# The convolution layer's load of t's rows, issued by SyncE instead of ScalarE

## The chip, the cores and the metric

The kernel runs on one core of a Trainium2 chip. A core has five engines that run side by side: TensorE (PE, with its weight loads PEld), VectorE (DVE), ScalarE (ACT), GpSimd (POOL) and SyncE (SP), which here only issues DMAs. Each engine works through its own queue of instructions in order and waits on semaphores for the others. SyncE, ScalarE and GpSimd can issue DMAs; a DMA that waits for something keeps all that stands behind it in that engine's queue waiting too. The metric is the device time of one execution in microseconds, the median of several runs.

## The reference

A feature map x of 1 x 256 x 256 x 128 float32 runs through four residual layers, each applied to a group-normalised input: triangle attention, two triangle multiplications, and a convolution layer. The change lies in the last, whose reference is

```python
def c1(t):   # a 1 x 9 convolution along a row, 128 channels to 1
    return lax.conv_general_dilated(t, w1, (1, 1), 'SAME', dimension_numbers=DN) + b1
def c2(t):   # a 128 x 128 product per pixel
    return jnp.einsum('bhwc,cd->bhwd', t, w2c) + b2
t = relu(c1(x))
y = jnp.concatenate([x[:, :1], x[:, 1:] + t[:, :-1]], axis=1)
u = relu(c1(y))
z_main = u + jnp.roll(y, 1, axis=1)
z = jnp.concatenate([z_main[:, :H - 2], u[:, H - 1:H] + y[:, H - 2:H - 1], y[:, H - 1:H]], axis=1)
v = relu(c2(z))
p = jnp.concatenate([z[:, :, :1], z[:, :, 1:] + v[:, :, :-1]], axis=2)
r = relu(c2(p))
q_main = r + jnp.roll(p, 1, axis=2)
```

The images t and u have one channel: each value is added to all 128 channels of a pixel. The output is x + q.

## The kernel before, in words

The first three layers end at about 2925 us; what follows is the convolution layer. It works on 32 groups of 8 image rows, channels on the partitions (1 MB a group). `for s in range(NR + 2)` at L1695 holds the order of all instructions, written out by hand; nothing is reordered by a planner.

Per group s, the main work is: `load9` (L1462) brings x into one of nine buffers; ScalarE writes x, scaled and moved by a row, into PSUM (`start_z`, L1580, tile `p_zp`, for group s + 1) and a copy of x into `p_q` (L1704); VectorE adds the one-channel part to make `p_z` (`finish_z`, L1595); TensorE multiplies by w2c twice (`p_half` and `q_half`, both L1601), VectorE takes the products (L1609, L1623), GpSimd adds the row-shifted p (`residual`, L1615 to L1617); `emit` transposes the group two steps back on TensorE (L1638, tile `p_pt`), ScalarE copies it out of PSUM (L1639, `p_o`) and SyncE stores it (L1640).

The one-channel images t and e (e is what u and t together add to a group's rows) are made in 16 blocks of 16 rows, one block per two groups, some groups ahead of their use. `taps` (L1468 on TensorE, `p_st` on ScalarE at L1472) makes the nine products of the 1 x 9 convolution, and SyncE writes them to DRAM with four DMAs (`sD`, L1477). `load_block` (L1487, two DMAs on SyncE) reads them back shifted so that adding nine numbers gives c1(x). A block b then passes these steps over two groups:

- even group: `sum_taps` on VectorE (L1509, L1510), `relu_t` on ScalarE (L1515), `shift_t` on GpSimd (L1519, L1522), and `keep_t` (L1527), a DMA from GpSimd's queue that writes t's rows to DRAM (`tD`).
- odd group: `load_t` (L1531), which reads t's rows back, one row up, into `p_t2`; `image_u` on VectorE (L1536), `relu_u` on ScalarE (L1540), `image_e` on GpSimd (L1545, which needs `p_t2`), and `keep_e` (L1551), a DMA from GpSimd's queue that writes e's rows to DRAM (`eD`).
- next even group: `load_e` (L1564), two DMAs from ScalarE's queue that read e's rows as single-partition rows; GpSimd broadcasts them to all partitions (`spread_e`, L1572) for `finish_z`.

So `load_t` must wait until the DMA of `keep_t` has landed, and `load_e` until that of `keep_e` has. In the profile the DMA issues of these queues show as SPq, ACTq and POOL. The PSUM tiles `p_zp`, `p_pp` (of `taps`) and `p_pt` share two buffers in turn, so the second `p_pt` of a group waits for `p_st` to free the buffer of `p_pp`.

The first three blocks are made ahead of or inside groups 0 and 1 with their DMAs on SyncE (`begin_image`, `end_image`); the loop's own loads of t are in the thirteen odd groups 3 to 27. `taps` runs in the loop's groups 2 to 25 and the x loads end with group 23's.

In an odd group before the change the queues hold, in this order:

- SyncE: x load of group s + 8, four `sD` writes, two `p_S` loads, output store.
- ScalarE: `p_pb` column, `p_zp`, `p_q`, **load_t**, `p_st`, two `p_o` copies, `relu_u`, a last column of `p_q`.
- GpSimd: `residual`, `spread_e`, `image_e`, the write of e.

Of the kernel before, what the change touches and what calls it, by code (L numbers as in the profile page):

```python
# [32 lines left out]
def kernel(ctx: ExitStack, tc: tile.TileContext, a: dict, out: bass.AP):  # L33
    nc = tc.nc
# [33 lines left out]
    tD = dram.tile([1, (N + 2) * NP], F32, name="tD")  # L68
# [1032 lines left out]
    with tc.tile_pool(name="x5", bufs=7) as x5_pool, tc.tile_pool(name="p5", bufs=2) as sb, tc.tile_pool(  # L1101
# [95 lines left out]
        for s in range(NSC):  # L1197
            b, j = divmod(s, KB)
# [248 lines left out]
    BR = 16  # L1447
    NB = N // BR
    BW = NP // 8
    LEAD = 6  # L1450
    with tc.tile_pool(name="p9", bufs=2) as sb, tc.tile_pool(name="p9psM", bufs=2, space=PSUM) as psM, tc.tile_pool(
# [7 lines left out]
        def load9(s):  # L1459
            if s < NR:  # L1460
                xs[s] = sb.tile([P, R, N], F32, name="p9_x", bufs=9)
                nc.sync.dma_start(xs[s], x3r[:, s * R : (s + 1) * R, :])  # L1462

        def taps(x, h0, n):

            pp = psX.tile([P, 2, CK], F32, name="p9_pp", tag="x")
            for c in range(n):
                nc.tensor.matmul(  # L1468
                    pp[32 * c : 32 * c + 32, 0, :], lhsT=w1f, rhs=x[:, 2 * c : 2 * c + 2, :], start=True, stop=True
                )  # L1470
            st = sb.tile([P, 2, N], F32, name="p9_st")
            nc.scalar.activation(  # L1472
                st[0 : 32 * n].rearrange("p h w -> p (h w)"), pp[0 : 32 * n, 0, :], AF.Identity, bias=s0[0 : 32 * n]
            )
            for c in range(n):
                at = 16 + (h0 + 2 * c + 1) * NP
                nc.sync.dma_start(  # L1477
                    sD_tap[:, at : at + 2 * NP].rearrange("k (h w) -> k h w", w=NP)[:, :, 0:N],
                    st[32 * c : 32 * c + TAPS],
                )  # L1480
# [13 lines left out]
        def load_block(b):  # L1494
            St = sb.tile([P, TAPS, 2 * BW + 8], F32, name="p9_S")
            load_taps(St, b * BR, 1, BW + 8, BW)
            load_taps(St, b * BR, 0, BW, 0)
            blocks[b] = dict(St=St)

        def image_rows(d, row, n=BR):  # L1500
            return d[:, row * NP : (row + n) * NP].rearrange("o (p w) -> p (o w)", w=BW)
# [10 lines left out]
        def relu_t(b):  # L1512
            k = blocks[b]
            k["t"] = sb.tile([P, BW + 8], F32, name="p9_t")
            nc.scalar.activation(k["t"], k["acc"], AF.Relu, bias=b1)  # L1515
# [10 lines left out]
        def keep_t(b, queue=nc.sync):  # L1526
            queue.dma_start(image_rows(tD, b * BR + 1), blocks[b]["t"][:, 4 : 4 + BW])  # L1527

        def load_t(b, queue=nc.sync):
            t2 = blocks[b]["t2"] = sb.tile([P, BW], F32, name="p9_t2")  # L1530
            queue.dma_start(t2, image_rows(tD, b * BR))  # L1531

        def image_u(b):
            k = blocks[b]
            k["u"] = sb.tile([P, BW], F32, name="p9_u")
            nc.vector.tensor_reduce(k["u"], k["prod"], AX.X, ALU.add)  # L1536
# [24 lines left out]
        def load_e(b, queue=nc.sync):  # L1561

            for s in range(2 * b, 2 * b + 2):
                queue.dma_start(  # L1564
                    row_e(s).rearrange("o (h w) -> o h w", w=N),
                    eD.rearrange("o (h w) -> o h w", w=NP)[:, s * R : (s + 1) * R, 4 : 4 + N],
                )

        def spread_e(s):
            if s < NR:  # L1570
                ebs[s] = sb.tile([P, SC], F32, name="p9_eb", bufs=1)
                nc.gpsimd.partition_broadcast(ebs[s], row_e(s))  # L1572

        def start_z(s):

            zps[s] = [psX.tile([P, H, N], F32, name="p9_zp", tag="x") for _ in range(2)]

            def take(lo, hi, src):
                h = lo // H
                nc.scalar.activation(zps[s][h][:, lo - h * H : hi - h * H, :], src, AF.Identity, bias=k0, scale=r3)  # L1580

            take(0, 1, xs[s - 1][:, R - 1 : R, :] if s else xe[:, 1:2, :])
            take(1, H, xs[s][:, 0 : H - 1, :])
            if s + 1 < NR:
                take(H, R, xs[s][:, H - 1 : R - 1, :])
            else:
                take(H, R - 2, xs[s][:, H - 1 : R - 3, :])
                take(R - 2, R, xs[s][:, R - 2 : R, :])

        def finish_z(s):  # L1590
            zs[s] = sb.tile([P, R, N], F32, name="p9_z", bufs=3)
            zf, eb = zs[s].rearrange("p h w -> p (h w)"), ebs.pop(s)
            for h, zp in enumerate(zps.pop(s)):
                hs = slice(h * H2, (h + 1) * H2)
                nc.vector.tensor_tensor(zf[:, hs], zp.rearrange("p h w -> p (h w)"), eb[:, hs], ALU.add)  # L1595
# [10 lines left out]
        def p_half(s, h):  # L1606
            rows_ = slice(h * H, (h + 1) * H)
            pm = product9(zs[s], h)
            nc.vector.scalar_tensor_tensor(  # L1609
                pbs[s][:, rows_, 1:N], pm[:, :, 0 : N - 1], kcol[:, 0:1], zs[s][:, rows_, 1:N], ALU.max, ALU.add  # L1610
            )

        def residual(s):
            q, pb = qs[s], pbs[s]
            nc.gpsimd.tensor_tensor(q[:, :, 1 : N - 2], q[:, :, 1 : N - 2], pb[:, :, 0 : N - 3], ALU.add)  # L1615
            nc.gpsimd.tensor_tensor(q[:, :, N - 2 : N], q[:, :, N - 2 : N], pb[:, :, N - 2 : N], ALU.add)
            nc.gpsimd.tensor_tensor(q[:, :, 0:1], q[:, :, 0:1], pb[:, :, N - 1 : N], ALU.add)  # L1617

        def q_half(s, h):
            rows_ = slice(h * H, (h + 1) * H)  # L1620
            q = qs[s]
            pm = product9(pbs[s], h)
            nc.vector.scalar_tensor_tensor(  # L1623
                q[:, rows_, 0 : N - 2], pm[:, :, 0 : N - 2], kcol[:, 1:2], q[:, rows_, 0 : N - 2], ALU.max, ALU.add
            )
            nc.vector.scalar_tensor_tensor(
                q[:, rows_, N - 2 : N - 1], pm[:, :, N - 1 : N], kcol[:, 1:2], q[:, rows_, N - 2 : N - 1],
                ALU.max, ALU.add,
            )
# [41 lines left out]
        def begin_image(b):  # L1671
            sum_taps(b)
            relu_t(b)
            shift_t(b)
            keep_t(b)
            load_t(b)

        def end_image(b):
            image_u(b)
            relu_u(b)  # L1680
            image_e(b)
            keep_e(b)
            load_e(b)
# [11 lines left out]
        for s in range(NR + 2):  # L1695
            b = s // 2 + 2
            load9(s + 8)
            if s < NR:
                pbs[s] = sb.tile([P, R, N], F32, name="p9_pb")
                nc.scalar.activation(pbs[s][:, :, 0:1], zs[s][:, :, 0:1], AF.Identity, bias=kcol[:, 0:1])  # L1700
                if s + 1 < NR:
                    start_z(s + 1)
                qs[s] = sb.tile([P, R, N], F32, name="p9_q", bufs=3)
                nc.scalar.activation(qs[s], xs[s], AF.Identity, bias=kcol[:, 2:3])  # L1704
            if s > 3 and s % 2 == 0 and b <= NB:
                load_e(b - 1, nc.scalar)
            if s > 1 and s % 2 == 1 and b < NB:
                load_t(b, nc.scalar)
            if s < NR:
                p_half(s, 0)  # L1710
                p_half(s, 1)
                del xs[s]
            if s < 2:
                begin_image(s + 1)
            if s + 1 < NR:
                finish_z(s + 1)
            if s < 2:
                end_image(s + 1)
            if 0 < s <= NR:
                q_half(s - 1, 0)  # L1720
                q_half(s - 1, 1)
                del pbs[s - 1], zs[s - 1]
            if s < NR:
                residual(s)
                spread_e(s + 2)
            if s < 2:

                for i in range(2):
                    taps(xs[4 + 2 * s + i], (4 + 2 * s + i) * R, 4)
                load_block(s + 2)  # L1730
            elif b < NB:
                sum_taps(b) if s % 2 == 0 else image_u(b)
            if s > 1 and s + LEAD < NR:
                taps(xs[s + LEAD], (s + LEAD) * R, 4)
            if s > 1 and s % 2 == 1 and b + 1 < NB:
                load_block(b + 1)
            if s > 1:
                emit(s - 2)
                if b < NB:
                    if s % 2 == 0:  # L1740
                        relu_t(b)
                        shift_t(b)
                        keep_t(b, nc.gpsimd)
                    else:
                        relu_u(b)
                        image_e(b)
                        keep_e(b, nc.gpsimd)
            if 0 < s <= NR:
                last = qs[s - 1][:, :, N - 1 : N]
                nc.scalar.activation(last, last, AF.Identity, bias=kcol[:, 1:2])  # L1750
# [182 lines left out]
```

## Time and profile before

| | us |
|---|---|
| median of 3 runs (3340.82 to 3342.47) | 3341.68 |
| the profiled execution, own time | 3345.7 |
| its span in the profile | 3342.8 |
| TensorE busy over the span | 3049.3 (91%) |
| VectorE | 2241.1 (67%) |
| ScalarE | 2038.4 (61%) |
| GpSimd | 1769.9 (53%) |

In the convolution layer's steady part, from 3080 to 3140 us, TensorE is busy for 54.22 of 60 us, VectorE for 44.28, ScalarE for 41.31, GpSimd for 47.06, and the DMA engines have a mean share of 0.72. From 3260 to 3320 us, TensorE is busy for 58.17 us of 60.

How to read it: the page gives busy times by engine and groups of instructions by line; the views used below are the list of waits (engine, tile and line that waited, what ended the wait, total us, times, longest), and the timeline (start, duration, engine, line, operation, output and input tile; in brackets the idle time of that engine just before, and what ended it). Buffer numbers are left out, so `p_t` in a DMA's name stands for `p_t` and `p_t2` alike. A DMA row gives the time of its issue; its transfer runs on afterwards. The granted clock is TensorE's share of full clock.

### The profile page before, as it was taken

To read this page: it belongs to the slowest core of one execution; us is meant where nothing else is said; L and a number is where in the kernel's file an instruction comes from. 1 tells how busy PE (TensorE), PEld (TensorE's weight loads), DVE (VectorE), ACT (ScalarE), POOL (GpSimd) and SP (SyncE) were. 2 spreads that over 40 slices of the span, in tenths; PEclk is the share of its full clock that TensorE was granted. 3 is DMA by queue.
4 is the path that set the end of the run, shared out by engine and by line. 5 is a ranking of instruction groups with operands and counts; after the bars stand their busy time and mean duration, and the time that the engine had idled before them with its cause. 6 is when DMAs were issued, how large, how long until landed. Compare 5 with 4: busy or idle time off the path is not lost. (4 is left out here: it accounts for less than half of the span.)

```text
span 3342.8 us, 51721 instructions
## 1 busy us (share of the span) xinstructions
PE 3049.3 (91%) x19780; PEld 1630.5 (49%) x19780; DVE 2241.1 (67%) x2532; ACT 2038.4 (61%) x2274; POOL 1769.9 (53%) x1012
## 2 busy tenths in 40 slices
PE   5678999999999999977897999999999999849998
PEld 5524555555555555532532344444799633314444
DVE  5626888888888888873555454545455688837776
ACT  3576777777777777744476544443444477736766
POOL 4054777777777777750286000000455588727776
PEclk8788999999999999998897999999999999969999
DMA  9882333333333333349599576775899899847774
GB/s 359 352 317 89 122 110 115 115 111 120 109 117 107 121 109 120 111 173 401 169 363 398 198 307 229 285 290 183 332 350 354 325 371 387 331 150 215 211 207 134
DMA packets 295169, 749.43 MB, mean 224 GB/s; under 512 B 71399, under 2 KB 142425, under 8 KB 245737
## 3 DMA queue, kind: packets, MB, share of 16 engines
q1 hardware_dynamic: 283799, 734.61, 61.1%
q0 software_dynamic: 8544, 9.99, 0.9%
q8 instruction: 158, 2.59, 0.3%
q10 hardware_dynamic: 2576, 1.48, 0.2%
q14 instruction: 92, 0.75, 0.1%
HBM read 458.34 MB, written 287.64 MB: 223 GB/s over the span
## 5 line engine op out<-in xcount | busy, mean ns | idle before, releaser
L565 DVE TENSOR_TENSOR p_e<-p_S,triT 128x1024 f32<-128x1024 f32 x512 | 609.1, 1211 | 144.3 <-PE p_S L555 144.3
L575 POOL TENSOR_TENSOR p_es<-p_e 128x1024 f32<-128x1024 f32 x256 | 603.5, 2368 | 123.6 <-issue 65.0
L573 ACT ACTIVATE p_e<-p_e,mbT 128x1024 f32<-128x1024 f32 x512 | 551.8, 1137 | 59.8 <-DVE p_e L565 59.6
L1172 PE MATMUL p_pm<-p_zn,wf 128*128 128x512 f32 x1040 | 449.2, 593 | 2.7 <-ACT p_a L1207 1.9
L540 PE MATMUL p_mm<-p_xn,w 128*128 128x512 f32 x768 | 406.9, 613 | 0.3 <-DVE p_v L535 0.3
L1172 PEld LDWEIGHTS p_pm<-p_zn,wf 128*128 128x128 f32 x1040 | 196.7, 190 | 255.3 <-issue 246.5
L555 PE MATMUL p_S<-p_q,p_k 32*128 32x256 f32 x4096 | 295.5, 401 | 3.3 <-DVE p_e L565 3.3
L1262 POOL MEMSET k<- 128x512 f32 x1 | 0.5, 521 | 507.0 <-DVE p_zn L1165 507.0
L555 PEld LDWEIGHTS p_S<-p_q,p_k 32*128 32x128 f32 x4096 | 186.0, 184 | 159.2 <-PE p_mm L531 91.7
L514 POOL TENSOR_TENSOR p_xn<-p_xn,p_rs 128x1024 f32<-128x1024 f32 x63 | 151.3, 2402 | 207.8 <-DMA p_rb<-rzD 111.3
L1891 PE MATMUL tp_z<-p_B,tp_at 128*128 128x256 f32 x1024 | 250.5, 388 | 0.7 <-DMA p_B<-bD 0.5
L588 PE MATMUL p_o<-p_e,p_v 128*32 128x256 f32 x4096 | 247.6, 382 | 0.0
L1293 POOL TENSOR_TENSOR k<-k,p_sq 128x512 f32<-128x512 f32 x128 | 163.1, 1274 | 158.9 <-ACT p_sq L1291 158.9
L1891 PEld LDWEIGHTS tp_z<-p_B,tp_at 128*128 128x128 f32 x1024 | 185.1, 191 | 23.2 <-DVE tp_at L1882 1.5
L1615 POOL TENSOR_TENSOR p_q<-p_q,p_pb 128x2024 f32<-128x2024 f32 x32 | 144.1, 4504 | 64.8 <-ACT p_q L1704 52.8
L540 PEld LDWEIGHTS p_mm<-p_xn,w 128*128 128x128 f32 x768 | 126.6, 191 | 105.6 <-issue 89.5
L1292 DVE TENSOR_TENSOR k<-tp_z,k 128x512 f32<-128x512 f32 x128 | 88.6, 692 | 127.0 <-ACT p_sq L1291 127.0
L588 PEld LDWEIGHTS p_o<-p_e,p_v 128*32 128x32 f32 x4096 | 120.0, 109 | 109.3 <-ACT p_g L546 41.5
L1289 ACT COPY p_K<-tp_z 128x512 f32<-128x512 f32 x128 | 75.0, 586 | 157.5 <-PE tp_z L1891 157.5
L546 ACT ACTIVATE p_g<-p_mm,bgh 128x512 f32<-128x512 f32 x128 | 88.0, 687 | 131.2 <-PE p_mm L540 131.2
L544 ACT ACTIVATE p_k<-p_mm,cqkg 128x512 f32<-128x512 f32 x128 | 88.1, 688 | 125.2 <-PE p_mm L540 124.9
L531 PEld LDWEIGHTS p_mm<-w,p_xn 128*128 128x128 f32 x1024 | 134.4, 191 | 61.1 <-issue 60.6
(379 smaller groups left out, 6040.6 us busy)
## 6 DMA issues: line engine op xcount, KB each, us to landing
p_x<-x2T SPq DMA_DIRECT2D x60, 1024.0 KB
x<-x1T SPq DMA_DIRECT2D x51, 1024.0 KB
p_x<-in_x_dram SPq DMA_DIRECT2D x32, 1024.0 KB
p_x<-xT SPq DMA_DIRECT2D x64, 512.0 KB
x2T<-x SPq DMA_DIRECT2D x32, 1024.0 KB
aD<-p_a SPq DMA_DIRECT2D x32, 1024.0 KB
bD<-p_b SPq DMA_DIRECT2D x32, 1024.0 KB
p_A<-aD SPq DMA_DIRECT2D x32, 1024.0 KB
```

The source lines that it names most:

```text
L514: nc.gpsimd.tensor_tensor(xn, xn, groups[g]["rs"], ALU.mult)
L531: nc.tensor.matmul(pm[:, k * D : (k + 1) * D], lhsT=t["xn"][:, b * P : (b + 1) * P], rhs=wf[:, 2 * D : 3 * D], start=True, stop=True,)
L540: nc.tensor.matmul(pm, lhsT=w, rhs=t["xn"][:, cs_], start=True, stop=True)
L555: nc.tensor.matmul(Ss[h // 2][:, h % 2, u, :], lhsT=t["k"][hp, r * N + u * P : r * N + (u + 1) * P], rhs=t["q"][hp, r * N : (r + 1) * N], ...
L565: nc.vector.tensor_tensor(e[:, :, 2 * p : 2 * p + 2, :].rearrange("p u h n -> p h u n"), Ss[p], triT[:, 2 * p : 2 * p + 2, :, :], ALU.add,)
L573: nc.scalar.activation(e[:, u, :, :], e[:, u, :, :], AF.Exp, bias=mbT[:, u, i : i + 1])
L575: nc.gpsimd.tensor_tensor(es, e[:, 0, :, :], e[:, 1, :, :], ALU.add)
L588: nc.tensor.matmul(t["o"][hp, r % 2, :], lhsT=t["v"][:, r * 2 + u, hp], rhs=e[:, u, h, :], start=(u == 0), stop=(u == 1),)
L1172: nc.tensor.matmul(pm[:, c, :], lhsT=wf2[:, i, :], rhs=zns[s][:, k * CK : (k + 1) * CK], start=True, stop=True)
L1293: nc.gpsimd.tensor_tensor(k2, k2, sq, ALU.add)
L1615: nc.gpsimd.tensor_tensor(q[:, :, 1 : N - 2], q[:, :, 1 : N - 2], pb[:, :, 0 : N - 3], ALU.add)
L1891: nc.tensor.matmul(pz[:, t, :], lhsT=at[:, u, t * P : (t + 1) * P], rhs=Bc[:, u, :], start=(u == 0), stop=(u == 1))
```

## The change

`load_t` is issued by SyncE in all places, and in the loop it moves up: it now stands right behind `load9`, the x load, in odd groups. Before, it stood in ScalarE's queue between the copy `p_q` and `p_st`. The write of t (`keep_t`), its waits and the tile it fills are the same. `begin_image` used SyncE before as well.

```diff
-        def load_t(b, queue=nc.sync):
+        def load_t(b):
             t2 = blocks[b]["t2"] = sb.tile([P, BW], F32, name="p9_t2")
-            queue.dma_start(t2, image_rows(tD, b * BR))
+            nc.sync.dma_start(t2, image_rows(tD, b * BR))
...
         for s in range(NR + 2):
             b = s // 2 + 2
             load9(s + 8)
+            if s > 1 and s % 2 == 1 and b < NB:
+                load_t(b)
             if s < NR:
...
             if s > 3 and s % 2 == 0 and b <= NB:
                 load_e(b - 1, nc.scalar)
-            if s > 1 and s % 2 == 1 and b < NB:
-                load_t(b, nc.scalar)
```

In an odd group SyncE's queue now holds: x load, load_t, four `sD` writes, two `p_S` loads, output store. The queues of TensorE and VectorE hold the same instructions in the same order, as GpSimd's does.

## The prediction

> **What bounds the kernel now.** The chain of work that ended last holds three pieces of about 1 us, so it says nothing of the changed stage. I read next the waits inside the last stage (2750 to 3343 us):
>
> ```profile
> ACT p_st L1472 <- DMA tD<-p_t: 42.7, 11, 4.7
> ...
> PE p_pt L1638 <- ACT p_st L1472: 22.2, 11, 2.8
> ```
>
> Eleven times ScalarE stands before its copy `p_st` until the write of t's rows has landed: that is load_t's wait, ahead of `p_st` in ScalarE's queue. Eleven times TensorE stands because `p_st` is late. The timeline of one pair of groups shows how (start, duration, engine, line; in brackets the idle time before and what ended it):
>
> ```profile
> 3146.87 0.69 ACT L1472 ACTIVATE p_st<-p_pp,s 128x512 f32<-128x512 f32 x1 [1.73 <-PE p_pp L1468]
> ...
> 3149.81 0.40 SPq L1640 DMA_DIRECT2D out_dram<-p_o  x1
> ...
> 3150.31 1.79 SPq L1462 DMA_DIRECT2D p_x<-x3T  x1
> ...
> 3152.96 1.99 ACT L1704 ACTIVATE p_q<-p_x,kcol 128x2048 f32<-128x2048 f32 x1
> ...
> 3153.46 0.57 POOL L1527 DMA_DIRECT2D tD<-p_t  x1
> ...
> 3155.04 4.50 POOL L1615 TENSOR_TENSOR p_q<-p_q,p_pb 128x2024 f32<-128x2024 f32 x1 [1.00 <-ACT p_q L1704]
> ...
> 3159.23 0.33 ACTq L1531 DMA_DIRECT2D p_t<-tD  x1
> ...
> 3159.68 0.69 ACT L1472 ACTIVATE p_st<-p_pp,s 128x512 f32<-128x512 f32 x1 [4.73 <-DMA tD<-p_t]
> ...
> 3160.39 1.36 SPq L1477 DMA_DIRECT2D sD<-p_st  x4
> 3160.42 0.86 PEld L1638 LDWEIGHTS p_pt<-ident,p_q 128*128 128x128 f32 x8 [3.07 <-ACT p_st L1472]
> ...
> 3163.06 1.03 SPq L1487 DMA_DIRECT2D p_S<-sD  x2
> ...
> 3163.48 0.56 POOL L1551 DMA_DIRECT2D eD<-p_e  x1 [0.30 <-POOL p_e L1545]
> ...
> 3164.18 1.06 SPq L1640 DMA_DIRECT2D out_dram<-p_o  x1
> ...
> 3165.29 2.34 SPq L1462 DMA_DIRECT2D p_x<-x3T  x1
> ...
> 3166.21 2.06 ACTq L1564 DMA_DIRECT2D p_er<-eD  x2
> ```
>
> Group 15 (odd) waits for t's rows, group 16 (even) for nothing but TensorE. TensorE's `p_z` products start at 3148.54, 3161.35 and 3171.12: 12.81 us for the odd group, 9.77 for the even one. From group 3 (3014.68) to group 25 (3260.84) eleven pairs take 246.16 us, 22.38 a pair. The trace also holds an odd group without the stall, group 25, where no x load is in flight:
>
> ```profile
> 3268.30 0.32 ACTq L1531 DMA_DIRECT2D p_t<-tD  x1
> 3268.93 0.69 ACT L1472 ACTIVATE p_st<-p_pp,s 128x512 f32<-128x512 f32 x1 [1.69 <-PE p_pp L1468]
> ...
> 3279.70 1.26 ACTq L1564 DMA_DIRECT2D p_er<-eD  x2
> 3281.06 1.93 ACT L1639 COPY p_o<-p_pt 128x1024 f32<-128x1024 f32 x2 [4.05 <-issue]
> ```
>
> It takes 9.77 us. The next group shows what can be late next: load_e, 4.45 us after its write (3275.25), holds ScalarE.
>
> **What the Trainium skill says.** "DMA: Bandwidth & Descriptors", Anatomy of one DMA: a DMA's wait is served by the issuing sequencer, not by the DMA engines; so the wait moves with the instruction, and what queues behind it changes. The same page, Queues, rings and completion order: a completion semaphore lands only after every earlier write of that DMA engine, across queues. The trace agrees: t's write lands 7.5 to 8.9 us after the x load ahead of it (mostly 7.9), whether issued 1.75 or 3.6 us behind it; x load 3196.30, landing 3204.23; x load 3128.78, landing 3136.65. "TensorE: Matmul & The Clock Gate", Part 1: after idleness the clock is halved. Here it was 0.55 and 0.50 in 2 us stretches at 3094, 3183 and 3228, after waits of 2.20, 1.98 and 1.75; the even groups then took 11.46, 11.36 and 10.99 instead of 9.77. That is inside the 22.38.
>
> **The change part by part.** It moves thirteen load_t (groups 3 to 27); nothing is added. ScalarE loses 13 issues of 0.33 us, 4.3 us, and the wait ahead of `p_st` with them. SyncE's queue gains both, behind the odd group's x load. Behind load_t there now stand four `sD` writes, two `p_S` loads, the output store and the even group's x load. Who waits: counted from the even `p_st`, the last `p_S` issue ends at 3.44 (x load) + 7.9 + 0.33 + 1.36 + 1.31 + 1.03 + 0.1 of gaps = 15.5 us, and the sum on VectorE that reads it comes at 1.67 (to the odd `p_z`) + 9.77 + 9.72 (3161.35 to 3171.07) = 21.2. At the stage's start two sets of `p_S` were in use 3.4 us after the first issue (2944.14 to 2947.57): hidden, with some 2 us left. Without this cover a late `p_S` would cost VectorE its lateness once a pair. An x load is used two groups later, some 20 us: hidden. load_t's reader on GpSimd (`p_e`) comes 7.35 us after the residual starts, about 2 us after load_t lands (1.84 us from issue to use at 2950.63): hidden.
>
> The pair cannot be shorter than its longest loop:
> (a) TensorE: 9.77 twice, 19.54.
> (b) From even `p_st` round to the next: to the end of the odd `p_q` 8.08 (3146.87 to 3154.95); residual start 0.09; to `p_e` 7.35 (3133.51 to 3140.86); to e's write 0.55; its landing 3.0 (median from issue; 2.7 to 3.5 where nothing large goes ahead); two load_e issues 1.4 (1.26 to 1.54 where not queued); `p_st` 0.1. Sum 20.6. Today load_e is hidden because the odd stall lets GpSimd catch up; afterwards it is the next late thing on ScalarE.
> (c) SyncE: odd x load to load_t's release 7.9; load_t 0.33, `sD` writes 1.36, their landing 1.31 (3161.75 to 3163.06), `p_S` 1.03, store 0.9 to 1.06, gaps 0.2, together 5.2; even x load to the next odd one 7.9. The last is there today: the built program gives the DMAs of SyncE and ScalarE eight completion semaphores in turn, so the odd x load waits until the even one, eight places earlier, has landed (3165.29 to 3173.21, 7.92). Sum 21.0.
>
> I take (c), 21.0; with landings of 7.5 to 8.3 it is 20.2 to 21.8. Its coupling back to the engines is the even group's GpSimd broadcast, which reads what load_e brought, and that lands with the even x load (3210.25, broadcast released at 3218.37). Saving: 11 x (22.38 - 21.0) = 15.2 us; TensorE's gap shrinks to 21.0 - 19.54 = 1.5 us, so I count no further clock loss. Groups 25 to 31 and the start stay. The profiled execution has span 3342.8 and own time 3345.7, so 3327.6 and 3330.5 there; it stood 4.0 above the median of the runs, 3341.68, from which I take 15.2: 3326.5, say 3327.
>
> **Rivals.** A change within 0.2%, 6.7 us, is about what a measurement of this kernel can't tell from none.
>
> *Everything hidden, TensorE is the bound.* For: group 25 at 9.77. Against: loops (b) and (c) are both longer. 11 x (22.38 - 19.54) = 31 us, 3310.
>
> *The wait comes back at load_e.* SyncE now stores earlier: x load at 3.44 after `p_st`, load_t 7.9 later at 11.3, store at 15.5; e's write comes at 16.07. Today the store comes from 0.13 before to 0.77 behind e's write, and landing takes 3 us. In group 26 it came 1.75 ahead and landing took 4.45. With 4.5 to 5, loop (b) is 22.1 to 22.6: -3 to +2 us, 3338 to 3344, no difference.
>
> *The other side: e's write is caught behind the x load too.* If store and x load get far enough ahead, its landing follows the x load as t's does: x load near 16, landing near 23.7, so 7.7 instead of 3.0. Loop (b) becomes 25.3: 11 x 2.9 = +32 us, 3374. The place is load_e on ScalarE in even groups. It decides once the store leads e's write by more than a lead between 0.13 (seen harmless) and 2.25 (where t's write was caught, 3195.81 and 3198.06); (b) alone would give 0.55. Against: loop (c), the slower, pushes the store back. Landing above about 5.5 is enough for over 0.2% slower.
>
> *The change doesn't act.* ScalarE could stall as long on something else at once; only load_t stands between `p_q` and `p_st` in odd groups, and the built ScalarE stream has thirteen entries fewer, so I give this nothing of its own.
>
> **How the numbers follow.** Loop (c) or (b) near 21: 0.54, its own range 3317 to 3336, of which the slow end touches the bound. TensorE bound: 0.07. Back at load_e with no difference: 0.18. Caught: 0.21. Faster by over 0.2%: 0.54 + 0.07 + 0.02 of the third case, 0.63; within 0.2%: 0.16; slower: 0.21. The range 3316 to 3352 leaves out most of the fourth case and the full gain, and keeps its mild forms.
>
> **What would show it.** Right: ScalarE's wait before `p_st` on t's write is gone; odd groups take 9.8; SyncE's wait for t's write is long (some 5 us each); even groups take 11 to 11.5, with ScalarE held before `p_st` by load_e; load_e is issued 3 us after e's write; sums on VectorE don't wait for `p_S`. Wrong: e's write landing in 5 us or more, TensorE waits above 2 us in even groups with halved clock behind them, or VectorE waiting for `p_S`.

## The result, and the profile after

| | kernel before | changed kernel |
|---|---|---|
| median, us | 3344.80 (20 runs, 3337.42 to 3355.17) | 3333.14 (20 runs, 3322.68 to 3343.70) |
| ratio to before, 95% interval | 1 | 0.9965 (0.9955 to 0.9974) |
| profiled execution: own time, span | 3345.7, 3342.8 | 3336.53, 3333.7 |

The changed kernel is faster by 11.7 us (8.7 to 15.1 by the interval). The prediction took 15.2 us off a median of three runs that was 3.1 us below the median of twenty; the distance of 6.6 us between 3326.5 and 3333.14 is those 3.1 and 3.5 us of saving that didn't come.

The view of waits from 2740 to 3334 us, first SyncE's own (engine, tile or line that waited, what ended the wait: total us, times, longest):

```profile
SPq L1531 <- DMA tD<-p_t: 83.3, 16, 12.9
...
SPq L1487 <- DMA sD<-p_st: 20.5, 28, 3.7
```

Before, the first of these lines was, from 2740 to 3343 us:

```profile
SPq L1531 <- DMA tD<-p_t: 15.5, 3, 12.7
```

Those three are the waits of the stage's start. So thirteen waits of together 67.8 us, 5.2 each, have come to SyncE. On the computing engines the stretch after the change shows:

```profile
ACT p_st L1472 <- issue: 18.2, 4, 5.0
...
PE p_pt L1638 <- ACT p_st L1472: 17.9, 10, 3.1
...
ACT p_st L1472 <- PE p_pt L1638: 11.8, 4, 3.3
POOL p_eb L1572 <- DMA p_er<-eD: 11.3, 7, 3.7
...
ACT p_st L1472 <- DMA p_er<-eD: 4.4, 1, 4.4
```

The line that carried the prediction, `p_st` waiting eleven times for `tD<-p_t`, is gone. But `p_st` still comes late: TensorE waits for it ten times, 17.9 us against 22.2 before, and ScalarE now stands before `p_st` in nine even groups, for reasons that the view calls "issue" (four), puts down to TensorE (four) or to load_e's DMA (one). GpSimd's broadcast `p_eb` waits longer for load_e's rows (11.3 us against 4.3), but what VectorE waits for the broadcast has hardly changed (12.7 against 11.3). The timeline says what holds `p_st`. A pair of groups, 13 and 14, as the changed kernel runs it where nothing disturbs it (start, duration, engine, line; in brackets the idle time before):

```profile
3114.06 0.69 ACT L1472 ACTIVATE p_st<-p_pp,s 128x512 f32<-128x512 f32 x1 [2.84 <-PE p_pt L1638]
...
3117.47 2.45 SPq L1462 DMA_DIRECT2D p_x<-x3T  x1
...
3123.83 0.69 ACT L1472 ACTIVATE p_st<-p_pp,s 128x512 f32<-128x512 f32 x1 [1.72 <-PE p_pp L1468]
...
3125.77 0.33 SPq L1531 DMA_DIRECT2D p_t<-tD  x1
...
3129.96 0.87 SPq L1640 DMA_DIRECT2D out_dram<-p_o  x1
3130.11 0.56 POOL L1551 DMA_DIRECT2D eD<-p_e  x1 [0.30 <-POOL p_e L1545]
...
3130.87 2.44 SPq L1462 DMA_DIRECT2D p_x<-x3T  x1
...
3132.82 1.70 ACTq L1564 DMA_DIRECT2D p_er<-eD  x2
...
3134.70 0.69 ACT L1472 ACTIVATE p_st<-p_pp,s 128x512 f32<-128x512 f32 x1 [2.80 <-PE p_pt L1638]
```

The odd group's `p_st` (3123.83) waits for TensorE alone, and load_t is issued 1.94 us after it, which holds up no computing engine. The even group's `p_st` (3134.70) stands behind the two issues of load_e, which end at 3134.52; load_e itself waited for e's write, 3130.11 to 3132.82, 2.71 us. From even `p_st` to even `p_st` it is 20.64 us; the two distances before this one are 20.70 and 20.68, the next is 21.17.

The same view four groups later, groups 17 and 18:

```profile
3159.28 2.68 SPq L1462 DMA_DIRECT2D p_x<-x3T  x1
...
3165.50 0.33 SPq L1531 DMA_DIRECT2D p_t<-tD  x1
...
3165.64 0.69 ACT L1472 ACTIVATE p_st<-p_pp,s 128x512 f32<-128x512 f32 x1 [1.72 <-PE p_pp L1468]
...
3166.35 1.36 SPq L1477 DMA_DIRECT2D sD<-p_st  x4
...
3170.22 1.01 SPq L1640 DMA_DIRECT2D out_dram<-p_o  x1
...
3171.28 2.21 SPq L1462 DMA_DIRECT2D p_x<-x3T  x1
...
3171.92 0.56 POOL L1551 DMA_DIRECT2D eD<-p_e  x1 [0.29 <-POOL p_e L1545]
...
3177.12 1.25 ACTq L1564 DMA_DIRECT2D p_er<-eD  x2
...
3178.55 0.69 ACT L1472 ACTIVATE p_st<-p_pp,s 128x512 f32<-128x512 f32 x1 [4.84 <-issue]
...
3179.29 1.97 PE L1638 MATMUL p_pt<-ident,p_q 128*128 128x128 f32 x8 [2.93 <-ACT p_st L1472]
```

Here load_t was released 6.22 us after the x load, not 8.30. It was through before `p_st` ended (3166.33), so it held nothing: the `sD` writes followed `p_st` at once. In group 13 they had to stand 1.68 us more, from the end of `p_st` at 3124.52 to 3126.20. All that stands behind them on SyncE came earlier by about as much: the store is 1.70 us ahead of e's write, where it was 0.15, and the even x load 0.64 us ahead. The write lands in 5.20 us, ScalarE stands 4.84 us, TensorE 2.93. Behind that wait the granted clock (the number after the five engines' busy times) is halved:

```profile
3180.00:3182.00 2.00, 2.00 (x8) 1.48 (x8) 0.00 (x0) 0.84 (x2) 1.89 (x1) 0.50 0.20 37
```

Groups 18, 20 and 22 run like this, e's write "caught" in the prediction's word, 13.74, 13.61 and 13.90 us long with landings of 5.20, 5.79 and 5.94. What tells them from the others is that hold: in the odd groups 3 to 15 the `sD` writes stood 0.58 to 2.33 us behind the end of `p_st`, and the store was at most 0.32 us ahead of e's write; in groups 17, 19 and 21 they stood 0.02 or 0.03 us, and it was 1.02 to 1.70 us ahead. The hold prevents the lead; without it the store need not run far ahead (0.33 us in group 23). The eleven pairs from group 3 to group 25, by the starts of `p_z` on TensorE:

| us | before | after | difference |
|---|---|---|---|
| eleven odd groups | 133.37 | 112.69 | -20.7 |
| eleven even groups | 112.79 | 130.23 | +17.4 |
| together | 246.16 | 242.92 | -3.2 |

Twenty of the microseconds taken out of the odd groups are there; seventeen came back in the even ones. This profiled execution gained only 3.2 us in the stage: another 5.6 us of its shorter span lie ahead of group 3, where both kernels do the same work. The start of group 3 scatters from 3008.25 to 3016.06 us over all kernels profiled here, and the change has no part in it. By the medians, 11.7 us over eleven pairs is 1.06 us a pair, so a typical pair takes some 21.3 us (an estimate from 22.38). The profiled execution, 3.4 us above its median, then holds more of the long pairs than most; that is argued from its time, since only one execution was profiled.

### The profile page after: what moved, and what is told of

Same layout as the page of the kernel before. It is cut to its first block, busy times and chain, and to the rows that moved or that the text cites. A ratio compares the mean times of both kernels' runs of the same rounds, so it can differ in the third digit from the quotient of the medians.

```text
span 3333.7 us, 51741 instructions
## 1 busy us (share of the span) xinstructions
PE 3044.9 (91%) x19780; PEld 1631.0 (49%) x19780; DVE 2241.9 (67%) x2532; ACT 2037.7 (61%) x2274; POOL 1769.6 (53%) x1012
```

## The experiments

The theory: the wait moved to SyncE and costs nothing there; what is left is load_e on ScalarE, which depends on where e's write falls among SyncE's large transfers. The rival: what remains of the gain's shortfall is the held SyncE queue itself. Every kernel was timed beside the kernel before, to which its ratio is; edits are to the changed kernel unless said otherwise.

**1. SyncE without load_t.** The wait and the DMA go out of the loop; `t2_kept` is the tile that the last load_t of the start filled, block 2's.

```diff
         def load_t(b):
-            t2 = blocks[b]["t2"] = sb.tile([P, BW], F32, name="p9_t2")
+            nonlocal t2_kept
+            t2 = t2_kept = blocks[b]["t2"] = sb.tile([P, BW], F32, name="p9_t2")
...
             if s > 1 and s % 2 == 1 and b < NB:
-                load_t(b)
+                blocks[b]["t2"] = t2_kept
```

> The changed kernel without the loop's thirteen loads of t; the loop's e rows are made with t's rows of block 2, so that part of the result is left out. No engine waits for t's write any more. Theory A (the pair is bounded by the way round through e's write and load_e on ScalarE, and e's write lands late once the store leads it by more than about 1 us): the store on SyncE comes about 1 us earlier without load_t's hold, so it leads e's write by more than 1 us in nearly every pair, e's write lands 5 to 6 us after issue, pairs take 23 to 24 us, time 3345 to 3365, no better than the kernel before. Theory B (load_t's hold on SyncE is what remains, TensorE is next): pairs near 20, time 3312 to 3322.

Measured: 3344.77 us, ratio 0.9996 (0.9987 to 1.0005): theory A's side, 0.2 us under its range. Freeing SyncE takes the whole gain away. The step from an odd group to an even one in its timeline (this kernel's lines stand one or two later):

```profile
3068.91 0.89 SPq L1642 DMA_DIRECT2D out_dram<-p_o  x1
...
3069.85 2.34 SPq L1463 DMA_DIRECT2D p_x<-x3T  x1
...
3070.63 0.56 POOL L1553 DMA_DIRECT2D eD<-p_e  x1 [0.29 <-POOL p_e L1547]
...
3076.13 1.27 ACTq L1566 DMA_DIRECT2D p_er<-eD  x2
...
3077.61 0.69 ACT L1473 ACTIVATE p_st<-p_pp,s 128x512 f32<-128x512 f32 x1 [5.19 <-issue]
```

The store leads e's write by 1.72 us, and the write takes 5.50 to land. Six of eleven even groups are like this (leads 0.72 to 1.76, landings 4.93 to 5.84); the even groups take up to 15.36 us. That is fewer than theory A had: it expected a lead of more than 1 us in nearly every pair and pairs of 23 to 24 us, and they took 22.60. In four of the other five the store was at most 0.35 us ahead; group 24, the fifth, has no x load near and its write landed in 4.27 us. So load_t's wait on SyncE isn't only free: it holds the store back until e's write is out.

**2. The even x load later.** Even groups issue their x load behind the `sD` writes, not at their head.

```diff
-            load9(s + 8)
+            if s < 2 or s % 2 == 1 or s + LEAD >= NR:
+                load9(s + 8)
...
                 taps(xs[s + LEAD], (s + LEAD) * R, 4)
+                if s % 2 == 0:
+                    load9(s + 8)
```

> The changed kernel with the even groups' x load issued behind the four sD writes of the same group instead of ahead of them; nothing is left out. Theory A: e's write then never has an x load ahead of it, lands in 2.6 to 4.4 us, the pairs of 24 us are gone, pairs near 20.7 throughout, 3324 to 3328. Theory B (the long pairs come from something else, such as TensorE's halved clock): no difference from the changed kernel, 3331 to 3335.

Measured: 3327.52 us, ratio 0.9948 (0.9935 to 0.9962). It lies in A's range, though its interval overlaps that of the changed kernel a little. Its timeline from group 13 to 14:

```profile
3125.55 0.33 SPq L1531 DMA_DIRECT2D p_t<-tD  x1
...
3129.47 0.56 POOL L1551 DMA_DIRECT2D eD<-p_e  x1 [0.30 <-POOL p_e L1545]
...
3129.85 0.94 SPq L1640 DMA_DIRECT2D out_dram<-p_o  x1
...
3132.61 1.75 ACTq L1564 DMA_DIRECT2D p_er<-eD  x2
...
3134.53 0.69 ACT L1472 ACTIVATE p_st<-p_pp,s 128x512 f32<-128x512 f32 x1 [3.43 <-PE p_pt L1638]
```

Not one write is caught: landings of 2.47 to 3.91 us, every odd group at 9.77, every even one between 11.27 and 12.29, 21.40 us a pair where theory A had 20.7. From even `p_st` to even `p_st` it is 21.27 here (3113.26 to 3134.53): the write leaves 0.16 us later than in the pair of the changed kernel shown above and lands 0.43 later. It is the prediction's case without a caught write, and still not TensorE's pair of 19.54, because load_e keeps its 3 us before `p_st`. The run doesn't say that the x load does the catching: load_t held the `sD` writes in all eleven odd groups (1.27 to 2.63 us), so the store was never more than 0.37 us ahead either.

**3. load_e on SyncE, ahead of the even x load.** The last DMA that waits leaves ScalarE too.

```diff
+            if s > 3 and s % 2 == 0 and b <= NB:
+                load_e(b - 1)
             load9(s + 8)
...
-            if s > 3 and s % 2 == 0 and b <= NB:
-                load_e(b - 1, nc.scalar)
```

> The changed kernel with load_e in the loop issued by SyncE ahead of the even group's x load instead of by ScalarE; nothing is left out. Theory A: load_e no longer holds ScalarE and holds the x load back until e's write has landed, so the pair falls toward TensorE's 19.54, to 19.6 to 20.2: 3314 to 3320. Theory C (SyncE's own round of waits, about 21, is the bound and load_e's wait lengthens it): pairs of 21 to 23, 3330 to 3350.

Measured: 3311.71 us, ratio 0.9893 (0.9879 to 0.9908), the best of all, a little beyond A's range. Its timeline at the same step:

```profile
3128.92 0.56 POOL L1551 DMA_DIRECT2D eD<-p_e  x1 [0.29 <-POOL p_e L1545]
...
3129.97 1.07 SPq L1640 DMA_DIRECT2D out_dram<-p_o  x1
...
3132.28 2.39 SPq L1564 DMA_DIRECT2D p_er<-eD  x2
3132.29 0.69 ACT L1472 ACTIVATE p_st<-p_pp,s 128x512 f32<-128x512 f32 x1 [1.69 <-PE p_pp L1468]
...
3134.73 0.42 SPq L1462 DMA_DIRECT2D p_x<-x3T  x1
```

`p_st` no longer stands behind load_e, and of the large transfers only the store, no x load, goes between e's write and load_e. Every even group takes 9.76 or 9.77, the odd ones 9.77 with three of 10.02 to 10.42: 19.65 us a pair, TensorE's bound within 0.11.

**4. The kernel before, its load_t later on ScalarE.** Another way to clear `p_st`: load_t stays on ScalarE, behind the `p_o` copies.

```diff
-            if s > 1 and s % 2 == 1 and b < NB:
-                load_t(b, nc.scalar)
...
                     else:
+                        load_t(b, nc.scalar)
                         relu_u(b)
```

> The kernel before with load_t left on ScalarE but moved from ahead of p_st to ahead of relu_u, behind the p_o copies; nothing is left out. Theory A: the wait on t's write is over before ScalarE gets there, but SyncE isn't held, so the store leads e's write by about 1 us or more as without load_t: pairs of 23 to 24, 3345 to 3365. Theory B (only ScalarE's stall before p_st ever mattered): pairs near 20 to 20.7, 3315 to 3326.

Measured: 3349.91 us, ratio 1.0009 (1.0000 to 1.0018), in A's range. The odd groups are at 9.77 again where the clock is full, and yet nothing is gained, as the timeline shows:

```profile
3096.28 0.94 SPq L1640 DMA_DIRECT2D out_dram<-p_o  x1
...
3097.27 2.31 SPq L1462 DMA_DIRECT2D p_x<-x3T  x1
...
3097.31 0.56 POOL L1551 DMA_DIRECT2D eD<-p_e  x1 [0.29 <-POOL p_e L1545]
...
3103.47 1.26 ACTq L1564 DMA_DIRECT2D p_er<-eD  x2
...
3104.86 0.69 ACT L1472 ACTIVATE p_st<-p_pp,s 128x512 f32<-128x512 f32 x1 [5.03 <-issue]
```

Seven writes have the store 1.03 to 1.75 us ahead and land in 5.41 to 6.16. That is experiment 1 by another road, with all work in place: with load_t off SyncE the store runs ahead and e's write is caught.

**5. Both edits of 1 and 2.** Meant to leave the store ahead of e's write and take the x load away, to tell which of them catches it.

> The changed kernel without the loop's thirteen loads of t (the e rows are made with t's rows of block 2, so that part of the result is left out) and with the even groups' x load behind the sD writes. The store still leads e's write by 1 us or more, but no x load stands behind the store. Theory A1 (the store alone makes e's write late, the x load adds to it): landing 4.2 to 4.5 us, pairs near 22, 3335 to 3342. Theory A2 (the x load alone makes it late): landing near 3 us, pairs near 20.7, 3323 to 3329. Theory A3 (the store alone does all of it): landing 5 to 6 us as without load_t, 3342 to 3350.

Measured: 3324.67 us, ratio 0.9941 (0.9926 to 0.9956), within the range of A2, but not for its reason. SyncE's waits, 2740 to 3311 us, hold a line that was 20.5 us in the changed kernel:

```profile
SPq L1488 <- DMA sD<-p_st: 59.2, 20, 5.8
```

The `sD` writes now land behind the x loads, the `p_S` loads wait for them, and the store behind these came 1.05 to 3.46 us *after* e's write. So this run doesn't tell the two apart. What it shows is the other end: in these eleven groups e's write landed in 1.76 to 3.06 us. The profiled execution, 3312.54 us, was the fastest of its six, so the median need not look like it.

**6. load_e on SyncE, behind the even x load.** As 3, with the two swapped.

```diff
             load9(s + 8)
+            if s > 3 and s % 2 == 0 and b <= NB:
+                load_e(b - 1)
...
-            if s > 3 and s % 2 == 0 and b <= NB:
-                load_e(b - 1, nc.scalar)
```

> The changed kernel with load_e issued by SyncE behind the even group's x load instead of ahead of it; nothing is left out. Theory A (ScalarE's hold at load_e is what bounds the changed kernel): most of the gain stays, pairs of 20 to 21, 3313 to 3326, even where e's write is caught behind the x load. Theory D (the gain came from holding the x load back): no better than the changed kernel, 3330 to 3340.

Measured: 3333.37 us, ratio 0.9959 (0.9946 to 0.9972), in the range of theory D and not of A: the gain of experiment 3 is gone, though ScalarE is as free as there. The even groups take 9.76 to 10.03, but odd ones go up to 16.90. From the view of waits, 2740 to 3334 us:

```profile
DVE p_z L1595 <- POOL p_eb L1572: 35.1, 12, 8.1
POOL p_eb L1572 <- DMA p_er<-eD: 33.4, 11, 6.3
```

Against 15.5 and 13.1 in experiment 3. load_e behind the x load brings its rows late, GpSimd's broadcast `p_eb` waits for them, VectorE for the broadcast, TensorE for VectorE. Both halves of experiment 3 count: ahead of the x load (against this run), and off ScalarE (against experiment 2, where no x load comes near e's write either and load_e is still on ScalarE, 3327.52 us).

**7. The kernel before with load_e on SyncE.** Experiment 3 without the change under study.

```diff
+            if s > 3 and s % 2 == 0 and b <= NB:
+                load_e(b - 1)
             load9(s + 8)
...
-            if s > 3 and s % 2 == 0 and b <= NB:
-                load_e(b - 1, nc.scalar)
             if s > 1 and s % 2 == 1 and b < NB:
                 load_t(b, nc.scalar)
```

> The kernel before, with load_t still on ScalarE, and load_e issued by SyncE ahead of the even group's x load; nothing is left out. Theory A: load_e was hidden in the kernel before, the stall on t's write in odd groups stays, odd groups stay near 11.8 us: 3338 to 3346, no gain. Theory E (load_e's place is worth as much by itself): 3312 to 3325.

Measured: 3341.34 us, ratio 0.9991 (0.9984 to 0.9998), in A's range. From its view of waits, 2740 to 3334 us:

```profile
ACT p_st L1472 <- DMA tD<-p_t: 41.3, 10, 4.9
```

load_t's wait is still there, and the pairs from group 3 to 25 take 246.34 us. Moving load_e alone gives next to nothing, moving load_t alone 0.35%, both 1.07%: in each case the wait that the other move removes stays.

## Why the prediction was right, and where its sizes were off

- *What it removes.* Right. The wait of `p_st` for t's rows is gone; eight of the twelve odd groups take 9.77 or 9.76, and the others have a granted clock of 0.50 for part of their time. "DMA: Bandwidth & Descriptors" of the Trainium skill, Anatomy of one DMA, says that the issuing sequencer serves a DMA's wait; SyncE's 67.8 us of new waits agree.
- *What the wait on SyncE holds up.* Right. The sums on VectorE wait for `p_S` four times both before and after (29.8 and 30.2 us), at the stage's start; GpSimd's `p_e` waits for load_t twice in both. That the hold also helps, the prediction had only as "pushes the store back", against its third rival; experiments 1 and 4 show that without it the whole gain is gone.
- *Loops (b) and (c).* (b) was worked out at 20.6 and measured 20.64 to 20.70 in three of the four undisturbed distances, 21.17 in the fourth; in the pair shown a landing of 2.71 for 3.0 and load_e of 1.70 for 1.4 cancel. Taking (c), 21.0, as the slower was wrong, and so was its reading that the odd x load waits for the even one. After the change every odd x load of groups 3 to 23 is issued within 0.10 us of the end of the store ahead of it; before, nine of the eleven were, within 0.11, and only those of groups 17 and 21 stood longer, 0.42 and 0.45. (The semaphore that they wait for is in the trace: it is that of load_e's first DMA, not that of the even x load.) So the last term is a distance and no wait: in groups 8 to 16 the even x load to the next odd one took 6.85 to 7.33 us, not 7.9, and the odd x load came 3.41 us after `p_st` (3114.06 to 3117.47), behind the store, which follows `p_o` and so `p_st`: the place where loop (b) puts it. The first term was 8.06 to 8.95 there, not 7.9, and the 5.2 between measured 5.10 to 5.37. The sum for the pair shown is 8.30 + 5.10 + 7.24 = 20.64. That 21.0 lies near the 21.3 estimated from the medians is therefore partly luck: it stands for a mixture of pairs near 20.7 and of longer ones with caught writes.
- *Landing of e's write, "3.0".* This is the term that was mis-sized, because one value stood for all pairs. It was 2.60 to 3.01 in six of the twelve even groups, 4.2 to 4.4 in three, 5.20 to 5.94 in three. The prediction treated "landing 3" and "caught" as cases of which one would hold; both occur within one execution, and with them most of the signs that it gave for being right and two of those for being wrong: landings above 5 us and TensorE's waits above 2 us in even groups with halved clock behind them. The distances of even `p_st` are 20.6 to 21.2 from group 8 to 16 and 22.7 to 24.3 from 16 to 24.
- *The opposing rival.* Its place (load_e on ScalarE) was right, and so was that store and x load then stand ahead of e's write. Experiments 1 and 4 bring it about in six and seven of eleven even groups, and the whole gain is gone. Its price was too high: landings of 4.9 to 6.2 us instead of 7.7 (by its own terms the x load follows the store of 15.5 by 1 us, so it is issued near 16.5 and not 16), since a caught write lands 5.8 to 6.6 us after the even x load where that went first, not 7.9. Its share of the pairs was what could not be read from the profile before.
- *"I count no further clock loss".* Wrong. Four odd groups behind caught writes or other long waits took 11.47, 10.52, 10.41 and 11.90 us, together 5.2 us over 9.77. The clock was 0.50 after a wait of 2.93 us, as "TensorE: Matmul & The Clock Gate" of the Trainium skill, Part 1, says of idleness in general; but the page gives an idle window of some 3.4 us, and here shorter waits were enough. Before, the three even groups that the prediction named lost 4.5 us, so the loss did not go away: it moved from even groups to odd ones.
- *TensorE is the bound.* Not reached by the change, but by experiment 3, at 3311.71 us against the 3310 that this rival was given.

Three things stay open. First, what starts a run of caught pairs. In groups 17 to 23 load_t is released 5.9 to 6.2 us after the odd x load, in earlier groups 7.2 to 8.95, and after each early release nothing holds the store. Once it has begun it may keep itself going: behind a caught write the odd x load is issued 11.6 to 11.8 us after the even one instead of some 7, so the two overlap less; but group 17, the first, had the usual distance of 6.85. Second, how much of the catching is the store's and how much the x load's: experiments 2 and 5 don't separate them, and the cases gathered below only bear on it. Third, how many caught pairs a typical execution holds.

## What to carry to other kernels

Put a DMA that must wait into the queue in which what stands behind it has slack, and then look for the next waiting DMA on the engine you freed: here the first move gave a third of what the two gave together. Ask also what becomes *early*: a wait that seemed pure loss kept a large store from overtaking a small write on which the next step hung. Issue the small dependent load ahead of the large one that needs nothing.

## What the runs showed of the hardware

How late e's write lands (from its issue to load_e's) goes with when the output store was issued relative to it. Over the profiles of both kernels and of experiments 1 to 5 and 7, the last block left out (in experiments 3 and 7 load_e stands behind the store on SyncE, so their landings may be shorter than this; in experiment 6, left out, it stands behind the x load too):

| store ahead of e's write, us | x load | landing, us |
|---|---|---|
| up to 0.46, or behind | any | 1.8 to 3.9, twice 4.2 to 4.4 |
| 0.58 to 1.93 | none within 5 us (10 cases) | 4.2 to 4.6 |
| 0.72 to 1.76 | 0.31 behind to 0.88 ahead of the write (16 cases) | 4.9 to 6.2 |

So the store alone goes with some 1.5 us over the usual 3, and the x load beside it with up to 1.5 more. The prediction looked for the step between 0.13 and 2.25 us of lead. In these runs a lead of 0.46 still went with 3.79 us and one of 0.58 with 4.59; but the two landings of 4.2 and 4.4, at leads of 0.33 and of 0.15 behind, show that the lead alone doesn't decide.
